# Causal masks of a state-space mixer by matmul: 64-token blocks against 32-token blocks

## The chip, the core and the metric

The kernel runs on one core of a Trainium2 chip. The metric is device time in microseconds, from the first to the last instruction of the program with the little that lies around it. Five engines matter: TensorE (PE, with the weight loads listed apart as PEld), VectorE (DVE), ScalarE (ACT), GpSimd (POOL) and SyncE (SP), which issues most of the DMAs.

## The reference

The input is 4 sequences of 1024 tokens with 512 features. It passes a mixer a, a feed-forward gate, a mixer b and the same gate again, each with a residual sum. Both mixers are state-space layers. With `a = A * dt` per token and head, the part that matters here is the decay between a token `s` and a later token `l` of a chunk, and its use:

```python
A_cs = jnp.cumsum(Ac, axis=-1)
L = jnp.exp(segment_sum(Ac))          # exp(sum of a over s < k <= l), 0 where l < s
Gm = jnp.einsum('bclhn,bcshn->bclsh', Cc, Bc)
M = Gm * jnp.transpose(L, (0, 2, 3, 4, 1))
Y_diag = jnp.einsum('bclsh,bcshp->bclhp', M, hc)
```

`segment_sum` holds minus infinity where `l < s`, so that a token takes nothing from later ones. Mixer a has 16 heads and mixer b 64. Mixer b is written in the reference as a scan over tokens; the kernel computes both in chunks of 128 tokens.

## The kernel before

The program is mixer a, the feed-forward part, mixer b, the feed-forward part again. A mixer runs over 4 sequences with 4 groups of two chunks of 128 tokens each: 16 groups, 32 chunks. While a group's chunks are worked off (`chunk`, L736), the projections of the next group run between them (`front`, L420: `convolve` with matmuls at L324 and taps on DVE at L451, `gate` with L518), and the normalisation of the one after it. The order of PE, DVE, ACT and POOL is written out by hand: `chunk` yields the us that it holds as covered, and a loop (L966 to L980) puts in pieces of `front` for that time. Each engine takes its instructions strictly in that order. Small matmuls (transposes, `pd`, `misc`) are slipped in between the large ones.

Per chunk, `decays(t)` (L755) makes the decays of 16 heads: once per chunk in mixer a, four times (t = 0 to 3) in mixer b, 160 times in all. It takes four PSUM banks `sg[r]`, each of 128 tokens `s` by 4 heads by 128 tokens `l`. First come the mask products (L762): an identity in bf16 times `later`, a matrix with -32768 where `l < s`, in two diagonal blocks of 64 by 64 tokens per bank, each with `start=True`. Then one matmul per bank (L772) adds `past` times `upto`, in f16: 21 rows for each r, at partitions 32 r to 32 r + 20. In rows 0, 1, 10 and 11 `upto` holds the sums of `a` up to `l` and `past` a constant; in rows 2 to 9 and 12 to 19 `past` holds the sums up to `s` and `upto` picks the head. The rows of sums are filled for every chunk by DMAs of `lay_sums` (L618). Row 20 is constant: 1 in `past` for `s >= 64` and -32768 in `upto` for `l < 64`, so the quarter of the square that lies wholly in the forbidden half is masked by the sums themselves. The quarter with `s < 64` and `l >= 64` needs no mask.

After it, ACT takes the exponential of each bank into L (L779), DVE multiplies L by Gm (`weigh`, L786) and PE multiplies it by the inputs (`inner`, L802) into one bank `py`, of which there is one. `open_y` (L833) puts the part from the state in first, `close_y` (L850) takes `py` out on DVE. `tail` (L646, L647) is the output projection of the chunk before. All PSUM tiles but `py` come from one pool of 7 banks, so a matmul into a new bank can wait for the engine that reads the bank's last use.

The constants are built once per mixer, ahead of the loop: `flags` (L271 to L284) are 11 reductions over the identity that give columns with ones at chosen partitions, and with these DVE fills two copies of `past` (L288, L291) and of `upto` (L294, L295), the latter per t. `past` is [128, TS, 128] and `upto` [128, TS, 4, 128] with TS = 1 in mixer a and 4 in mixer b. Other DVE work stands around them in the same queue: the scaling of the convolution's weights (L244), of `Ab` (L247, L249) and of the output weights (L252), which wait for their DMAs.

## Time and profile before

| | |
|---|---|
| median of 3 runs | 3233.39 us (3232.75 to 3239.16) |
| profiled execution | 3234.7 us, its span 3233.0 us |
| granted TensorE clock | 0.965 mean |
| PE busy | 2890.7 us (89%), 18372 matmuls |
| DVE busy | 2035.7 us (63%) |
| ACT, POOL busy | 1246.2 us (39%), 782.5 us (24%) |
| mask products L762, mixer b / a | 1024 / 256 matmuls, mean 277 / 279 ns |
| sums L772, mixer b / a | 512 / 128 matmuls, mean 386 / 390 ns |

The matmuls of mixer a run from about 72 to 1240 us, those of mixer b from about 1422 to 2951; the feed-forward parts lie between and after. In a row of the timeline, the numbers are the start in us from the span's start and the us from the first start to the last end of a run of like instructions; an idle time in brackets names what ended it. Matmuls are pipelined, so the mean of one is longer than the distance from one to the next, which is read from the starts. In a row of a group of instructions, busy time and mean of one come first, and then the idle time of that engine just ahead of it. A wait is put down to the last instruction that it waited for.

### The profile page before, as it was taken

How to read it: one execution, taken by the hardware profiler on the slowest of the kernel's cores; microseconds unless marked ns; L12 is line 12 of the kernel's file. 1: busy time of each engine (PE TensorE's matmuls, PEld its weight loads, DVE VectorE, ACT ScalarE, POOL GpSimd, SP SyncE). 2: the span in 40 equal slices, each digit the busy share in tenths (PEclk: the TensorE clock that was granted, in tenths of full speed). 3: DMA queues.
4: the chain of work that ended last, by engine and by line, in shares of the span. 5: the costliest groups of instructions: out<-in, count | busy, mean ns of one | idle time of the engine just before them, and what ended most of it. 6: DMA issues, size and time to landing. Idle time of an engine off the chain costs nothing. (4 is left out here: it accounts for less than half of the span.)

```text
span 3233.0 us, 48622 instructions
## 1 busy us (share of the span) xinstructions
PE 2890.7 (89%) x18372; PEld 1916.6 (59%) x18372; DVE 2035.7 (63%) x4326; ACT 1246.2 (39%) x2848; POOL 782.5 (24%) x842
## 2 busy tenths in 40 slices
PE   6999999999999988988999888989888989997973
PEld 5666666666666653356666666666666666664331
DVE  4666566655556642267766687776687676674288
ACT  2333333333333323334443444344444444343242
POOL 1122121122211221022222223221222222221068
PEclk9999999999999998999999999999999999998987
DMA  3000000000000025420000000000000000023143
GB/s 110 15 16 15 16 16 16 22 16 16 15 16 22 16 67 176 168 86 12 29 19 25 19 26 24 19 22 22 19 25 22 17 25 19 22 68 125 33 147 117
DMA packets 100521, 135.97 MB, mean 42 GB/s; under 512 B 40792, under 2 KB 44376, under 8 KB 100288
## 3 DMA queue, kind: packets, MB, share of 16 engines
q1 hardware_dynamic: 86944, 100.92, 10.1%
q10 hardware_dynamic: 9216, 16.78, 1.4%
q0 software_dynamic: 4128, 15.16, 1.3%
q8 instruction: 146, 2.39, 0.3%
q14 instruction: 87, 0.71, 0.1%
HBM read 96.09 MB, written 36.72 MB: 41 GB/s over the span
## 5 line engine op out<-in xcount | busy, mean ns | idle before, releaser
L324 PE MATMUL pc_b<-xnT_b,w_in_b 128*128 128x259 f32 x1280 | 360.3, 408 | 22.2 <-DVE u_b L451 22.2
L786 DVE TENSOR_TENSOR L_b<-L_b,Gm_b 128x1024 f32<-128x1024 f32 x256 | 317.4, 1282 | 2.9 <-ACT L_b L779 2.9
L646 PE MATMUL pout_a<-w_out_a,h_a 128*128 128x512 f32 x512 | 285.6, 650 | 27.3 <-DVE u_a L451 27.3
L324 PE MATMUL pc_a<-xnT_a,w_in_a 128*128 128x259 f32 x1152 | 309.2, 393 | 0.0
L324 PE MATMUL pz_a<-xnT_a,w_in_a 128*128 128x256 f32 x1024 | 300.2, 407 | 8.9 <-ACT xnT_a L413 8.9
L324 PE MATMUL pz_b<-xnT_b,w_in_b 128*128 128x256 f32 x1024 | 292.4, 394 | 0.7 <-ACT xnT_b L413 0.7
L324 PEld LDWEIGHTS pc_b<-xnT_b,w_in_b 128*128 128x128 f32 x1280 | 230.7, 201 | 101.6 <-issue 37.3
L1141 PE MATMUL g_ps<-gw,xnT_f 128*128 128x512 f32 x512 | 253.2, 639 | 39.4 <-ACT xnT_f L1138 25.5
L779 ACT ACTIVATE L_b<-seg_b 128x512 f32<-128x512 f32 x512 | 262.7, 598 | 65.9 <-PE seg_b L772 65.1
L646 PE MATMUL pout_b<-w_out_b,h_b 128*128 128x512 f32 x512 | 278.5, 635 | 0.0
L451 DVE SCALAR_TENSOR_TENSOR u_b<-pc_b,cw_b,u_b 128x256 f32<-128x256 f32 x480 | 231.7, 483 | 70.7 <-ACT u_b L447 59.3
L802 PE MATMUL py_b<-L_b,hdt_b 128*32 128x128 f32 x4096 | 162.7, 294 | 118.0 <-DVE L_b L786 116.7
L451 DVE SCALAR_TENSOR_TENSOR u_a<-pc_a,cw_a,u_a 128x256 f32<-128x256 f32 x432 | 208.3, 482 | 53.0 <-ACT u_a L447 41.6
L324 PEld LDWEIGHTS pc_a<-xnT_a,w_in_a 128*128 128x128 f32 x1152 | 193.3, 190 | 68.5 <-issue 22.9
L802 PEld LDWEIGHTS py_b<-L_b,hdt_b 128*32 128x32 f32 x4096 | 109.5, 115 | 161.7 <-issue 81.7
L1141 PEld LDWEIGHTS g_ps<-gw,xnT_f 128*128 128x128 f32 x512 | 97.4, 201 | 169.2 <-issue 116.4
L324 PEld LDWEIGHTS pz_a<-xnT_a,w_in_a 128*128 128x128 f32 x1024 | 168.6, 193 | 47.1 <-ACT xnT_a L413 9.3
L447 ACT ACTIVATE u_a<-pc_a,cb_a,cw_a 128x256 f32<-128x256 f32 x144 | 81.3, 564 | 283.9 <-PE pc_a L324 220.3
L324 PEld LDWEIGHTS pz_b<-xnT_b,w_in_b 128*128 128x128 f32 x1024 | 166.3, 190 | 37.1 <-issue 18.2
L854 POOL TENSOR_TENSOR h_b<-h_b,z_b 128x256 f32<-128x256 f32 x128 | 90.6, 729 | 386.4 <-ACT sq_b L853 386.4
L824 DVE TENSOR_TENSOR yo_a<-po_a,ea_a 128x512 f32<-128x512 f32 x56 | 36.1, 686 | 220.4 <-PE po_a L820 220.4
L647 PEld LDWEIGHTS ssq_a<-ones,sq_a 128*128 128x128 f32 x512 | 98.4, 194 | 127.8 <-issue 115.9
(310 smaller groups left out, 5275.3 us busy)
## 6 DMA issues: line engine op xcount, KB each, us to landing
x_f<-xa SPq DMA_DIRECT2D x32, 256.0 KB
sgd<-sg SPq DMA_DIRECT2D x32, 256.0 KB
sgl<-sgd SPq DMA_DIRECT2D x32, 256.0 KB
x_b<-xa SPq DMA_DIRECT2D x32, 256.0 KB
xb<-x_b ACTq DMA_DIRECT2D x32, 256.0 KB
x_f<-xb SPq DMA_DIRECT2D x32, 256.0 KB
x_g<-xb SPq DMA_DIRECT2D x32, 256.0 KB
out<-x_g SPq DMA_DIRECT2D x32, 256.0 KB
```

The source lines that it names most:

```text
L324: nc.tensor.matmul(*args, **kw)
L447: nc.scalar.activation(u, ps[:, 0:GT], AF.Identity, bias=cb[:, j : j + 1], scale=cw[:, j, 0:1])
L451: nc.vector.scalar_tensor_tensor(u, ps[:, k : k + GT], cw[:, j, k : k + 1], u, ALU.mult, ALU.add)
L646: nc.tensor.matmul(pout, f.hs[e // 2][:, e % 2, cols], w_out[:, e, :], **on)
L647: nc.tensor.matmul(ssq[:, 0:1], sqs[e // 4][:, e % 4, :], ones[:, 0:1], **on)
L779: nc.scalar.activation(L[:, r], sg[r0 + r], AF.Exp)
L786: nc.vector.tensor_mul(Lr, Lr, Gm.unsqueeze(1).to_broadcast([P, 2 * HB, P]))
L802: nc.tensor.matmul(py[cg * CT : (cg + 1) * CT, e % 4, :], hdt[:, h // HC, u : u + HC, :], Ls[half][:, r, hq, :], start=not started[cg], st ...
L824: nc.vector.tensor_mul(heads_of(tmp), heads_of(po), over_head(el[:, half * HALF : (half + 1) * HALF], P, HALF))
L854: nc.gpsimd.tensor_mul(yh, yh, zs[half * 2 + r][:, :, cols])
L1141: nc.tensor.matmul(ps, xnT[:, k, :], gw[:, k, :], start=(k == 0), stop=(k == KD - 1))
```

## The change

The mask products now come in four diagonal blocks of 32 by 32 tokens per bank instead of two of 64 by 64: 16 matmuls of 128 columns per call of `decays` instead of 8 of 256. What lies in a 64-token block off these diagonal blocks and is forbidden (`s` in 32 to 63 with `l` in 0 to 31, and `s` in 96 to 127 with `l` in 64 to 95) is masked by two more constant rows, 21 and 22, of `past` and `upto`. The sums' matmuls therefore read 23 rows instead of 21. `flags` gets two more columns, `past` two more steps per copy and `upto` two more steps per copy and t. Line numbers below L305 stay as they were.

```diff
-            flags = wk.tile([P, 2 * HB + 3], F32, tag="flags", name=f"flags_{m.name}")
+            flags = wk.tile([P, 2 * HB + 5], F32, tag="flags", name=f"flags_{m.name}")
...
-                + [slice(20, 21)]
+                + [slice(20 + n, 21 + n) for n in range(3)]
...
+            steps = [(slice(0, 64), slice(64, P)), (slice(0, 32), slice(32, 64)), (slice(64, 96), slice(96, P))]
+            steps = [(flags[:, 2 * HB + 2 + n : 2 * HB + 3 + n], *at) for n, at in enumerate(steps)]
...
-                nc.vector.tensor_scalar(past[:, :, 64:], past[:, :, 64:], row20, None, ALU.add)
+                for on, _, s in steps:
+                    nc.vector.tensor_scalar(past[:, :, s], past[:, :, s], on, None, ALU.add)
...
-                    nc.vector.scalar_tensor_tensor(
-                        upto[:, t, :, :64],
-                        row20.unsqueeze(1).to_broadcast([P, HB, 64]),
-                        MASKED,
-                        upto[:, t, :, :64],
-                        ALU.mult,
-                        ALU.add,
-                    )
+                    for on, l, _ in steps:
+                        to = upto[:, t, :, l]
+                        spread = on.unsqueeze(1).to_broadcast([P, HB, l.stop - l.start])
+                        nc.vector.scalar_tensor_tensor(to, spread, MASKED, to, ALU.mult, ALU.add)
...
-                        for q in range(2):
-                            at = slice(64 * q, 64 * q + 64)
+                        for q in range(4):
+                            at = slice(32 * q, 32 * q + 32)
                             nc.tensor.matmul(
                                 sg[r][at, :, at],
                                 ident16[at, at],
-                                later[at, at].unsqueeze(1).to_broadcast([64, HB, 64]),
+                                later[at, at].unsqueeze(1).to_broadcast([32, HB, 32]),
...
-                        rows = slice(32 * r, 32 * r + 21)
+                        rows = slice(32 * r, 32 * r + 23)
```

More of the change, by code (lines that the diff above doesn't have):

```diff
@@ L274, in mixer @@
                 + [slice(10 * lo, 10 * lo + 2) for lo in (0, 1)]
-                + [slice(20, 21)]
+                + [slice(20 + n, 21 + n) for n in range(3)]
             ):
                 nc.vector.tensor_reduce(flags[:, i : i + 1], eye[:, :, at], mybir.AxisListType.XY, ALU.add)
-            heads4, first2, row20 = flags[:, :HB], flags[:, 2 * HB : 2 * HB + 1], flags[:, 2 * HB + 2 :]
+            heads4, first2 = flags[:, :HB], flags[:, 2 * HB : 2 * HB + 1]
             nc.vector.scalar_tensor_tensor(
```

## The prediction

> **What bounds the kernel now.** I read the granted clock first (0.965 on the one core, 1.0 in the stretches used below), then the busy digits: PE is busy 89% of the span, DVE 63%, ACT 39%, POOL 24%. PE is the fullest engine, but its matmul time is not evenly the limit, so next came the waits of PE alone, to see where it stands still in the two mixers:

> ```profile
> PE py_b L802 <- DVE L_b L786: 116.7, 75, 5.2
> PE pout_a L646 <- DVE u_a L451: 27.3, 14, 3.0
> PE pc_b L324 <- DVE u_b L451: 22.2, 15, 1.5
> ```

> The columns are us in total, times, longest. There are 16 groups of two chunks in each mixer, so a row with 14 or 15 times is a wait that comes back in nearly every group, always for DVE. A PE instruction that ends earlier ahead of such a wait makes only the wait longer. So I laid one group of mixer b out in time: PE's rows with the mask products (L762) and each wait behind them (columns: start, us, instruction, idle time before it).

> ```profile
> 1846.78 0.62 PE L762 MATMUL seg_b<-later,ident 64*64 64x256 bf16 x8
> ...
> 1861.70 0.62 PE L762 MATMUL seg_b<-later,ident 64*64 64x256 bf16 x8
> ...
> 1866.37 0.62 PE L762 MATMUL seg_b<-later,ident 64*64 64x256 bf16 x8
> ...
> 1870.63 0.64 PE L802 MATMUL py_b<-L_b,hdt_b 128*32 128x128 f32 x16 [0.92 <-DVE L_b L786]
> ...
> 1891.39 2.21 PE L802 MATMUL py_b<-L_b,hdt_b 128*32 128x128 f32 x32 [5.24 <-DVE L_b L786]
> ...
> 1897.74 0.62 PE L762 MATMUL seg_b<-later,ident 64*64 64x256 bf16 x8
> 1898.29 0.40 PE L772 MATMUL seg_b<-upto_b,past_b 21*128 21x512 f16 x4
> ...
> 1900.06 0.35 PE L647 MATMUL ssq_b<-ones,sq_b 128*128 128x1 f32 x2 [0.31 <-DVE u_b L451]
> ...
> 1911.49 0.62 PE L762 MATMUL seg_b<-later,ident 64*64 64x256 bf16 x8
> 1912.05 0.40 PE L772 MATMUL seg_b<-upto_b,past_b 21*128 21x512 f16 x4
> 1913.92 0.68 PE L324 MATMUL pc_b<-xnT_b,w_in_b 128*128 128x259 f32 x2 [1.48 <-DVE u_b L451]
> ```

> What the reader is to see: from 1846.78 to 1861.70 PE has no idle time, while in DVE's rows a z_b of L518 stands at 1862.40 and waits for the gate that PE made just before 1861.70. From there DVE runs with one short gap (1.02 at 1874.01, itself behind DVE's own Gm_b) to 1898.4, and PE waits for it three times. So PE leads in one stretch of the group and DVE in the next.

> **The change part by part.** (1) The mask products. A narrow window around 1898 shows the pairs of one block one by one:

> ```profile
> 1897.87 0.49 PE L762 MATMUL seg_b<-later,ident 64*64 64x256 bf16 x6
> ...
> 1898.09 0.27 PE L762 MATMUL seg_b<-later,ident 64*64 64x256 bf16 x2
> ```

> The first of the eight starts at 1897.74, the third at 1897.87, the seventh at 1898.09: two pairs take 0.22, so a pair takes 0.109 us for 256 columns in each of two 64x64 tiles at once. The sums (L772) start 0.20 after the last pair: 0.109 of it is that pair, 0.09 the switch of the array from 64 rows to 32. The four sums of 386 ns each start together and end within 0.40. After the change there are four quads of 128 columns in four 32x32 tiles instead of four pairs of 256 columns. If a quad takes half a pair's time, a block saves 4 x (0.109 - 0.055) = 0.22 us. No row of before shows 32x32 tiles, so the bounds are: a quad that takes 0.109 saves nothing; quads that run one matmul after the other cost 16 x 0.055 = 0.87 against 0.44, a loss of 0.44; at best the switch to the sums goes too, since both would then be 32 rows high, and a block saves 0.31. I take 0.22 by the two nearest rows: the sums run in four row tiles at once, and at 1883.12 the 32 L802 matmuls (four column tiles, 128 columns of f32) take 1.01 until the next start, less a switch of 0.10 some 0.114 per quad. The eight 259-column f32 matmuls of L324 at 1909.64 take 1.85 to the next start, 0.09 of it a switch: 0.22 each, twice as long per column as bf16, so L802's quad runs at the full rate of its columns. Two more rows in the sums (23 for 21) cost nothing: their time goes by 512 columns; past and upto keep their shape and the DMAs that fill the rows of sums are unchanged, so SP's queue is too.

> [...] By the row, both tiles of a pair write the bank sg[r] and still start and end together (eight matmuls of 0.27 in 0.62). [...]

> (2) Which of the 160 blocks count. Mixer b, eight blocks per group: those at 1861.70 and 1866.37 end in the waits of 0.92 and (1872.84) 1.56 for L_b, the one at 1879.36 in the 5.24, the one at 1897.74 in the 0.31, that at 1911.49 in the 1.48, that at 1918.19 in waits of 0.61 and 0.49. In each, DVE's run began earlier than the block, so the saving turns into wait. Two are left: the last of the second chunk (1929.70; PE then runs to 1941 with no wait above 0.2 while DVE waits 1.34 for py_b) and the first of the next group (as at 1846.78). That is 32 in 16 groups, and I add 2 for the last chunks, where no projections of a next group fill PE. Mixer a, two blocks per group: PE has no wait between the first (505.18) and 521.2, where DVE's next run starts; the second is followed by the wait that the second row above counts:

> ```profile
> 541.41 0.62 PE L762 MATMUL seg_a<-later,ident 64*64 64x256 bf16 x8
> 541.97 0.39 PE L772 MATMUL seg_a<-upto_a,past_a 21*128 21x512 f16 x4
> ...
> 544.05 1.10 PE L646 MATMUL pout_a<-w_out_a,h_a 128*128 128x512 f32 x2 [1.69 <-DVE u_a L451]
> ```

> So 16 in a, 50 in all: 50 x 0.22 = 11.0 us less.

> (3) Setup on DVE, once per mixer. Mixer b at 1419 to 1432:

> ```profile
> 1419.24 0.87 DVE L277 TENSOR_REDUCE flags_b<-ident 128x1 f32<-128x8 f32 x11
> ...
> 1422.17 0.18 DVE L244 TENSOR_SCALAR cw_b<-cw_b 128x40 f32<-128x40 f32 x1 [0.33 <-DMA cw_b<-in_L_attn_b_conv_w]
> ...
> 1430.94 0.75 DVE L295 SCALAR_TENSOR_TENSOR upto_b<-flags_b,upto_b 128x256 f16<-128x256 f32 x2
> 1431.73 0.06 DVE L308 MEMSET sign_b<- 64x1 f32 x1
> 1431.82 0.36 DVE L488 TENSOR_TENSOR v_b<-pd_b,dtb_b 128x64 f32<-128x64 f32 x2
> ```

> DVE goes without a gap worth naming from here to 1464.8; PE's pd_b for the L488 was done by 1428.3, PE waits 8.77 for xn_b at 1453 and 1.46 for parts_b at 1461, and the first sums at 1473 wait for the DMA behind two_b. So DVE work added here moves everything after it. Added: 2 reductions at 0.07 (0.87 for 11) = 0.15; 4 more past steps of 128 elements, from L291 (next start 0.15 after 64 elements, 0.20 after 256) at 0.17 = 0.7; 16 more upto steps of 128 elements. L295 gives 0.335 from start to start for 256 elements, about 0.07 fixed and 0.27 for the elements, so 0.20 for 128: 3.2; where each waits for the one before (four dependent L542 of 128 take 1.27) 0.32: 5.1. Together 4.0 to 6.0; I take 4.5. DVE idles 0.33 for cw_b and 0.91 for Ab_b (1425.20) among them, and what stands ahead of those takes their place: 1.2 off, so 3.3 more, between 2.8 and 6.0. In mixer a the same comes to 10 instructions, some 1.7 us, at 6 to 9 us. What hides them is ACT: the second copy of xnT stands behind the exponential of Ab_a, which waits for its DMA until 20.1, so 8 us of cover; without it they would cost the 1.7.

> Sum: 3234.7 (the profiled execution: span 3233.0 and 1.7 around it) - 11.0 + 3.3 = 3227.0. That execution is 1.3 above the median of the runs, so on the median's scale 3225.7.

> **The rivals.** (A) Issue bounds the quads. Each matmul brings its own weight load, and no row keeps up 20 matmuls faster than L802's 28 ns each; 16 x 28 = 0.45, as long as the pairs now. For it: nothing shorter is sustained in this trace. Against: the sums' four loads and matmuls start within about 0.01 of each other. Then only the setup is left: +3.3, 3236.7. (B) Fewer blocks count: DVE and PE are close where I took PE to lead (L3's second half is weighed at 1937.28, its product starts near 1938.2, so 0.9 in hand, which speaks against). With 32 blocks: -7.0 + 3.3, 3229.7. [...] (D) Every block counts, 160 x 0.22 = 35, less 3.3: 3201.6; the waits shown speak against it.

> **How the numbers follow.** Forecast 0.60, A 0.15, B 0.08, C 0.11, D 0.06. About 0.2%, 6.5 us, is what a measurement of this kernel can tell from no change. The forecast's own range: saving per block 0.20 to 0.31, 46 to 54 blocks, setup 2.8 to 6.0, so 3220 to 3230; some three quarters of it lie below 3226.9. Faster: 0.45 from it and D's 0.06, 0.51. Same: the rest of it, A and B, 0.37. Slower: C and a little of A, 0.12. Leaving out C and D (0.17), the range is 3219 to 3239.

> **What would show it.** L762 with 2560 matmuls of 32*32 32x128, a block some 0.34 from its first mask to its sums instead of 0.55, and 0.66 to the matmul after the sums instead of 0.88. The wait of py_b for L_b grows from 116.7 by some 14 (four blocks per group), that of pout_a from 27.3 by 3. The last upto step of mixer b ends about 3.3 later after its first reduction. [...] The prediction is wrong if the groups move by other than 0.44 in b and 0.22 in a, or if the DMA waits do not cover part of the setup.

## The result, and the profile after

| | before | after |
|---|---|---|
| median of 22 runs each | 3236.72 us (3229.52 to 3242.47) | 3244.88 us (3233.86 to 3253.35) |
| ratio to before, 95% interval | | 1.0022 (1.0013 to 1.0030) |
| profiled execution: its time, its span | 3234.7, 3233.0 us | 3247.1, 3245.4 us |
| granted TensorE clock, profiled execution | 0.965 | 0.957 |
| granted TensorE clock, mean of the runs that list it (before: those beside the experiments) | 0.963 | 0.958 |

The kernel became slower by 0.22%, some 8 us on the medians. The forecast was 3225.7 against the 3233.39 known then, faster by 0.24%, with a range that ended at 3239: sign and range were both wrong.

Where the time went is read from the starts of four fixed points in the two traces, in us: the first and the last block of mask products in each mixer, and on DVE the first reduction of `flags_b` and the first z_b (L518) of mixer b. "Half" counts the stretches of 3.41 us with a granted clock of 0.5, in mixer a between 150 and 1170 us, in mixer b between 1500 and 2900 us.

| | before | after | difference | forecast |
|---|---|---|---|---|
| mixer a, first to last block (half) | 1124.2 (5) | 1134.7 (13) | +10.5 | -3.5 |
| setup of b, first reduction to first z_b | 12.85 | 16.68 | +3.8 | +3.3 |
| mixer b, first to last block (half) | 1474.2 (23) | 1473.8 (29) | -0.4 | -7.5 |
| the rest of the span | 621.7 | 620.2 | -1.5 | 0 |

Mixer a, where the forecast had the smaller saving, makes most of the loss; mixer b gains almost nothing; the setup is as forecast. The page of the changed kernel, its head and its clock digits:

```profile
span 3245.4 us, 51214 instructions
PE 2892.6 (89%) x19652; PEld 1917.7 (59%) x19652; DVE 2040.9 (63%) x4358; ACT 1245.7 (38%) x2848; POOL 781.4 (24%) x842
PEclk9999999999999998998999999999999999998997
```

PE has 1280 more matmuls and the same busy time as before (2890.7): busy time does not show the loss, since matmuls at half clock count as busy too (PE is busy for 3.42 of the 3.42 us of the stretch at clock 0.50 from 545.13, shown below). Now the waits of PE that the prediction read (us in total, times, longest):

```profile
PE py_b L802 <- DVE L_b L786: 121.7, 82, 5.3
PE pout_a L646 <- DVE u_a L451: 26.5, 14, 2.9
PE pc_b L324 <- DVE u_b L451: 25.5, 15, 1.7
```

The first grew by 5.0 where +14 was forecast, the second fell by 0.8 where +3 was forecast: a block that gets shorter ahead of a wait lengthens the wait, so part of these blocks did not get shorter. The timeline of PE in one group of mixer b shows which (start, us, instruction, idle time before it):

```profile
1858.62 0.40 PE L762 MATMUL seg_b<-later,ident 32*32 32x128 bf16 x16
1858.96 0.65 PE L772 MATMUL seg_b<-upto_b,past_b 23*128 23x512 f16 x4
1859.54 1.13 PE L646 MATMUL pout_b<-w_out_b,h_b 128*128 128x512 f32 x2
...
1873.58 0.40 PE L762 MATMUL seg_b<-later,ident 32*32 32x128 bf16 x16
1873.91 0.39 PE L772 MATMUL seg_b<-upto_b,past_b 23*128 23x512 f16 x4
1874.24 0.70 PE L324 MATMUL pc_b<-xnT_b,w_in_b 128*128 128x259 f32 x2
1874.78 0.38 PE L707 MATMUL misc_b<-Cc_b,Bc_b 128*128 128x128 f32 x2
...
1903.27 2.22 PE L802 MATMUL py_b<-L_b,hdt_b 128*32 128x128 f32 x32 [5.30 <-DVE L_b L786]
...
1909.91 0.40 PE L762 MATMUL seg_b<-later,ident 32*32 32x128 bf16 x16
1910.24 0.65 PE L772 MATMUL seg_b<-upto_b,past_b 23*128 23x512 f16 x4
```

The block at 1873.58 is what the prediction drew: 0.33 from the first mask to the sums, 0.66 to the next matmul. The blocks at 1858.62 and 1909.91 are the first ones (t = 0) of a chunk. Their masks are as short, but the four sums, which in 155 of the 160 blocks of before started within 0.01 of each other and ended within some 0.40, now take 0.65, and the next matmul comes 0.92 after the first mask: later than the 0.88 of before. Over all groups the medians from the first mask to the next matmul are, in us:

| block | before | after |
|---|---|---|
| mixer b, t = 0, both chunks of a group | 0.88 | 0.92 |
| mixer b, t = 1 and 2 of the first chunk, t = 2 and 3 of the second | 0.88 | 0.66 |
| mixer b, t = 3 of the first chunk: waits for DVE fall between its masks | 1.90 | 1.83 |
| mixer b, t = 1 of the second chunk: a wait for DVE follows | 2.44 | 2.44 |
| mixer a, first chunk of a group (its only block) | 0.88 | 0.84 |
| mixer a, second chunk: a wait for DVE follows | 2.64 | 2.63 |

The instructions of the block at 1909.91, with those of PE's sequencer, show why (start, length in ns):

```
1909.904  first weight load of the masks, the first mask at 1909.906
1909.928  51  sequencer, L772 EVENT_SEMAPHORE
1910.039  51  sequencer, L772 EVENT_SEMAPHORE
1910.094      last of the 16 masks starts
1910.164  51  sequencer, L772 EVENT_SEMAPHORE
1910.241      first sum starts
1910.272      second sum starts
1910.290  51  sequencer, L772 EVENT_SEMAPHORE
1910.398      third sum starts
1910.416  51  sequencer, L772 EVENT_SEMAPHORE
1910.524      fourth sum starts
```

The sums' waits for the DMAs of their rows stand as instructions of their own in PE's sequencer. There are 304 of them at L772 in both kernels, of 51 ns each in the median; in the group looked at, five belong to the first block of each chunk and none to the others, as the rows of `past` and `upto` are filled once per chunk. In the block of before at 1897.74 they ran from 1895.476 to 1896.131, some two microseconds ahead of the block: there the sequencer was that far ahead of the array. Ahead of the waits in the block stand 16 instructions there, 8 weight loads and 8 masks of 256 columns. Behind the 32 instructions for masks of 128 columns the sequencer reaches the first of the waits 0.02 us after the first mask has started, and the last sums then come 0.126 apart behind it. That, and the clock in mixer a, are the two causes that the experiments had to test.

The setup on DVE, from the timeline of the changed kernel:

```profile
1428.43 1.00 DVE L277 TENSOR_REDUCE flags_b<-ident 128x1 f32<-128x8 f32 x13
...
1431.74 0.18 DVE L244 TENSOR_SCALAR cw_b<-cw_b 128x40 f32<-128x40 f32 x1 [0.92 <-DMA cw_b<-in_L_attn_b_conv_w]
...
1444.24 0.82 DVE L302 SCALAR_TENSOR_TENSOR upto_b<-flags_b,upto_b 128x256 f16<-128x256 f32 x3
...
1445.11 0.68 DVE L518 SCALAR_TENSOR_TENSOR z_b<-tz_b,pz_b 128x512 f32<-128x512 f32 x1
```

From the first reduction to the first z_b it is 16.68 against 12.85. Of the two idle times for DMAs that I let the new work cover (0.33 for cw_b, 0.91 for Ab_b), the second is gone, but the first grew to 0.92: 0.3 in all was covered, not 1.2, so the work itself came to 4.1, below my 4.5.

### The profile page after: what moved, and what is told of

Same layout as the page of the kernel before. It is cut to its first block, busy times and chain, and to the rows that moved or that the text cites. A ratio compares the mean times of both kernels' runs of the same rounds, so it can differ in the third digit from the quotient of the medians.

```text
span 3245.4 us, 51214 instructions
## 1 busy us (share of the span) xinstructions
PE 2892.6 (89%) x19652; PEld 1917.7 (59%) x19652; DVE 2040.9 (63%) x4358; ACT 1245.7 (38%) x2848; POOL 781.4 (24%) x842
## 3 DMA queue, kind: packets, MB, share of 16 engines
q10 hardware_dynamic: 9216, 16.78, 1.4%
## 5 line engine op out<-in xcount | busy, mean ns | idle before, releaser
L324 PE MATMUL pc_b<-xnT_b,w_in_b 128*128 128x259 f32 x1280 | 363.0, 409 | 25.5 <-DVE u_b L451 25.5
L646 PE MATMUL pout_a<-w_out_a,h_a 128*128 128x512 f32 x512 | 297.6, 674 | 26.5 <-DVE u_a L451 26.5
L786 DVE TENSOR_TENSOR L_b<-L_b,Gm_b 128x1024 f32<-128x1024 f32 x256 | 317.3, 1281 | 2.7 <-ACT L_b L779 2.7
L324 PE MATMUL pc_a<-xnT_a,w_in_a 128*128 128x259 f32 x1152 | 311.3, 395 | 0.0
L324 PE MATMUL pz_a<-xnT_a,w_in_a 128*128 128x256 f32 x1024 | 300.1, 407 | 8.7 <-ACT xnT_a L413 8.7
L324 PEld LDWEIGHTS pc_b<-xnT_b,w_in_b 128*128 128x128 f32 x1280 | 232.6, 202 | 106.0 <-issue 39.1
L324 PE MATMUL pz_b<-xnT_b,w_in_b 128*128 128x256 f32 x1024 | 292.4, 394 | 0.7 <-ACT xnT_b L413 0.7
L646 PE MATMUL pout_b<-w_out_b,h_b 128*128 128x512 f32 x512 | 278.5, 635 | 0.0
L451 DVE SCALAR_TENSOR_TENSOR u_b<-pc_b,cw_b,u_b 128x256 f32<-128x256 f32 x480 | 231.5, 482 | 71.8 <-ACT u_b L447 60.4
L802 PE MATMUL py_b<-L_b,hdt_b 128*32 128x128 f32 x4096 | 163.9, 296 | 123.7 <-DVE L_b L786 121.7
L451 DVE SCALAR_TENSOR_TENSOR u_a<-pc_a,cw_a,u_a 128x256 f32<-128x256 f32 x432 | 208.3, 482 | 52.6 <-ACT u_a L447 41.6
L324 PEld LDWEIGHTS pc_a<-xnT_a,w_in_a 128*128 128x128 f32 x1152 | 194.9, 191 | 69.2 <-issue 22.9
L802 PEld LDWEIGHTS py_b<-L_b,hdt_b 128*32 128x32 f32 x4096 | 110.5, 116 | 167.4 <-issue 80.9
L324 PEld LDWEIGHTS pz_a<-xnT_a,w_in_a 128*128 128x128 f32 x1024 | 168.6, 193 | 47.1 <-ACT xnT_a L413 9.1
L324 PEld LDWEIGHTS pz_b<-xnT_b,w_in_b 128*128 128x128 f32 x1024 | 166.4, 190 | 37.1 <-issue 17.6
L647 PEld LDWEIGHTS ssq_a<-ones,sq_a 128*128 128x128 f32 x512 | 102.7, 202 | 134.5 <-issue 122.5
```

The source lines that it names most:

```text
L324: nc.tensor.matmul(*args, **kw)
L451: nc.vector.scalar_tensor_tensor(u, ps[:, k : k + GT], cw[:, j, k : k + 1], u, ALU.mult, ALU.add)
L646: nc.tensor.matmul(pout, f.hs[e // 2][:, e % 2, cols], w_out[:, e, :], **on)
L647: nc.tensor.matmul(ssq[:, 0:1], sqs[e // 4][:, e % 4, :], ones[:, 0:1], **on)
L786: nc.vector.tensor_mul(Lr, Lr, Gm.unsqueeze(1).to_broadcast([P, 2 * HB, P]))
L802: nc.tensor.matmul(py[cg * CT : (cg + 1) * CT, e % 4, :], hdt[:, h // HC, u : u + HC, :], Ls[half][:, r, hq, :], start=not started[cg], st ...
```

## The experiments

The theories, as they came up. S: the first blocks lose the saving because the sums' waits are no longer met ahead of time. H: mixer a got slower through the granted clock. Rivals: that the setup is the loss; that the shorter blocks gain nothing anywhere; that something else in a's blocks is slower.

**One part alone.** The setup alone: three steps of masking and 23 rows, but blocks of 64; then the blocks of 32 with their rows in one mixer only.

```diff
 # e1_setup_alone, against the changed kernel
-for q in range(4):
-    at = slice(32 * q, 32 * q + 32)
+for q in range(2):
+    at = slice(64 * q, 64 * q + 64)
...
-        later[at, at].unsqueeze(1).to_broadcast([32, HB, 32]),
+        later[at, at].unsqueeze(1).to_broadcast([64, HB, 64]),
 # e2_b_alone ("b") and e2x_a_alone ("a"), against the changed kernel
+BLK = 32 if m.name == "b" else 64
+if BLK == 64:
+    steps = steps[:1]
...
-for q in range(4):
-    at = slice(32 * q, 32 * q + 32)
+for q in range(P // BLK):
+    at = slice(BLK * q, BLK * q + BLK)
...
-        later[at, at].unsqueeze(1).to_broadcast([32, HB, 32]),
+        later[at, at].unsqueeze(1).to_broadcast([BLK, HB, BLK]),
...
-rows = slice(32 * r, 32 * r + 23)
+rows = slice(32 * r, 32 * r + 20 + len(steps))
```

> The setup and the 23 rows alone; the mask products stay in 64-token blocks. Theory (three terms: DVE setup, sums' waits in the queue, clock gate in mixer a): from the first reduction of flags_b to the first z_b 16.7 us as in the changed kernel (12.85 before), every block from first mask to sums 0.557 and 0.88 long as before, mixer a from its first block to its last within 3 us of before's 1124 us, the total about +3.8, 0.1% slower. Rival (the 23 rows or the rows' extra masks disturb the sums): first blocks longer than 0.88 with the sums spread over 0.28 us, and mixer a about 10 us longer without any 32-token block.

> 32-token blocks in mixer b alone; mixer a has before's 64-token blocks and 21 rows. Theory (the clock gate in mixer a makes the loss): mixer a back at 1124 us within 3 us, with about 5 half-clock windows between 150 and 1170 us instead of 13; setup of b +3.8; mixer b within 2 us of before (the first blocks of the chunks 0.92, the others 0.66); total +2 to +5 against before. Rival (the loss of some 10 us comes with the new blocks wherever they are, by issue or by switches of the array): mixer b shows it too and the total stays near +8.

> 32-token blocks in mixer a alone, mixer b as before. Theory (the loss sits in mixer a's clock): mixer a 1130 to 1136 us with 9 or more half-clock windows, setup of b 12.85 as before, mixer b 1474 us; total +4 to +10 against before, so most of the whole change's loss. Rival (the loss is spread over setup and mixer b, and mixer a's windows are chance of one execution): total within 3 us of before.

| | mixer a (half) | setup of b | mixer b (half) | ratio to before, 95% |
|---|---|---|---|---|
| e1_setup_alone | 1124.3 (6) | 16.70 | 1476.3 (25) | 0.9998 (0.9988 to 1.0007) |
| e2_b_alone | 1128.5 (9) | 16.80 | 1476.8 (30) | 1.0002 (0.9992 to 1.0012) |
| e2x_a_alone | 1131.4 (11) | 13.17 | 1474.7 (23) | 1.0013 (0.9999 to 1.0027) |

The setup of 3.8 us is there in each trace with the new steps in b, but not in e1's total: +3.8 was expected, and the interval, -3.9 to +2.3 us, leaves it out. What made up for it is not shown. In e1's trace the blocks take 0.88 as before and the sums stay together, so the 23 rows do not spread them; nor is one sum longer with 23 rows, 384 ns in the median in mixer b of the changed kernel for 385 before. With blocks of 32 in b alone the total is that of before. The blocks in a alone are slower in the point estimate, with an interval that just reaches one. In mixer a the same code gave 1124.2, 1124.3 and 1128.5 us with 5, 6 and 9 half-clock stretches (before, e1, e2), the changed code 1134.7 and 1131.4 with 13 and 11: a's time follows the number of stretches, which differs between executions too, and a single trace needs care here.

**The sums first.** The sums open the accumulation and the masks close it. The sums' waits then have no block of masks between the projections and themselves.

```diff
 # e3_sums_first, against the changed kernel: in decays(t)
+for r in range(4):
+    rows = slice(32 * r, 32 * r + 23)
+    nc.tensor.matmul(sg[r], past[rows, t, :], upto[rows, t], start=True, stop=False, skip_group_check=True)
 for r in range(4):
     for q in range(4):
...
-            start=True,
-            stop=False,
+            start=False,
+            stop=True,
-for r in range(4):
-    rows = slice(32 * r, 32 * r + 23)
-    nc.tensor.matmul(sg[r], past[rows, t, :], upto[rows, t], start=False, stop=True, skip_group_check=True)
```

> The changed kernel with the order within a block turned round: the four sums first (they open the bank), then the sixteen mask products. Theory (the sums' waits for DMA stand behind 32 mask instructions, so the sequencer comes to them too late): the four sums start within 0.02 us of each other in all blocks with landed DMAs, blocks of 0.66 instead of 0.92 or 0.84, 0.25 us less in 32 blocks on PE's stretch, 5 to 8 us in all as far as the clock gate lets them through; half-clock windows in mixer a as many as in the changed kernel (13) or more. Rival (the spread of the sums comes from the array, four row tiles with 23 rows after 32x32 tiles): the spread of 0.28 stays in the first blocks of the chunks, and so does the time.

Ratio to before 0.9997 (0.9986 to 1.0008); mixer a 1134.1 (10), setup 16.77, mixer b 1463.5 (25). The timeline of PE in e3, one group of mixer b with the first block of each chunk at 1856.31 and 1908.66:

```profile
1856.31 0.39 PE L761 MATMUL seg_b<-upto_b,past_b 23*128 23x512 f16 x4
1856.64 0.40 PE L767 MATMUL seg_b<-later,ident 32*32 32x128 bf16 x16
1856.97 1.13 PE L646 MATMUL pout_b<-w_out_b,h_b 128*128 128x512 f32 x2
...
1871.01 0.40 PE L761 MATMUL seg_b<-upto_b,past_b 23*128 23x512 f16 x4
1871.33 0.40 PE L767 MATMUL seg_b<-later,ident 32*32 32x128 bf16 x16
1871.67 0.70 PE L324 MATMUL pc_b<-xnT_b,w_in_b 128*128 128x259 f32 x2
...
1908.66 0.40 PE L761 MATMUL seg_b<-upto_b,past_b 23*128 23x512 f16 x4
1908.99 0.40 PE L767 MATMUL seg_b<-later,ident 32*32 32x128 bf16 x16
1909.32 1.13 PE L646 MATMUL pout_b<-w_out_b,h_b 128*128 128x512 f32 x2
```

The first blocks take 0.66 to the next matmul like the rest, and mixer b is 10.7 us shorter than before, 10.3 shorter than after. The only blocks whose length differs clearly from after are the first ones of the two chunks of each group, by 0.26 each. From these blocks to the next ones it is 0.30 and 0.18 less on average, which in 16 groups is 7.7 of the 10.3. So S holds for b; the 2.6 left over are not explained. Mixer a is as long as in after: its loss is another one. The block of each group's first chunk is even longer there, 1.16 to the next matmul, as its sums now wait openly for the DMAs of the rows.

**The clock in mixer a.** The timeline of the changed kernel at the wait behind a's second block, the place that the prediction showed of before at 541.41:

```profile
541.85 0.40 PE L762 MATMUL seg_a<-later,ident 32*32 32x128 bf16 x16
542.18 0.74 PE L772 MATMUL seg_a<-upto_a,past_a 23*128 23x512 f16 x4
544.48 1.40 PE L646 MATMUL pout_a<-w_out_a,h_a 128*128 128x512 f32 x2 [1.55 <-DVE u_a L451]
...
545.96 2.06 PE L646 MATMUL pout_a<-w_out_a,h_a 128*128 128x512 f32 x2
...
549.39 1.10 PE L646 MATMUL pout_a<-w_out_a,h_a 128*128 128x512 f32 x2
```

After the wait a pair of L646 takes 1.40 and then 2.06, until it is back at the 1.10 that before had at once (at 544.05). The busy times by stretches of 3.41 us, here and one group later (length, then busy us of PE, PEld, DVE, ACT, POOL with counts, the granted clock, DMA share, GB/s):

```profile
541.72:545.13 3.41, 1.86 (x23) 0.80 (x22) 3.27 (x6) 2.70 (x8) 0.97 (x1) 1.00 0.00 0
545.13:548.55 3.42, 3.42 (x9) 2.13 (x8) 2.83 (x10) 1.59 (x4) 0.00 (x0) 0.50 0.00 0
616.81:620.23 3.42, 1.78 (x23) 0.80 (x22) 2.07 (x5) 2.71 (x9) 0.00 (x0) 1.00 0.00 0
620.23:623.64 3.41, 3.41 (x9) 1.75 (x7) 3.02 (x10) 1.78 (x4) 0.00 (x0) 0.50 0.00 0
```

In the clock records of both traces (64 and 92 of them) every change between 1.0 and 0.5 lies a whole number of 3.413 us from the others, so the clock is read here by stretches of 3.41 us on one grid. If each matmul is counted for as long as its columns stream (259 columns of f32 in 0.22, 128 of bf16 in 0.056), the full-clock stretches of mixer a that were followed by half clock streamed some 0.29 to 0.40 of the time in before and 0.32 to 0.47 in after; of those that were not, the emptiest had 0.40 and 0.43. In the two together, every such stretch under 0.40 was followed by half clock and none over 0.47; between, both occur. This count gives no sharper limit, and the stretch with a's second block and the wait of 1.7 behind it, some 0.43 at 541.72 in after, lies in between. Whether the shorter masks pushed it over is for the experiments to show.

Two more things follow from the grid. Eleven of the 13 half-clock stretches of after begin 75.1 us apart, at 319.9, 394.9, 470.0, 545.1 and so on to 1070.8, once per group: 75.1 is 22 stretches. A slowed group thus ends with its wait at the same place of the grid, and the next one is slowed too. And a stretch at clock 0.5 costs up to half of its 3.41 us, 1.7 us by my estimate, if PE sets the pace. The experiment: make the masks of a's second block several times. They are written with `start=True`, so the result is that of the last time; the additional products fill the wait.

```diff
 # e4_after_fill_a, against the changed kernel: in decays(t)
-for r in range(4):
-    for q in range(4):
+for _ in range(7 if m.name == "a" and c == 1 else 1):
+    for r in range(4):
+        for q in range(4):
 # e5_before_fill_a: the same in the kernel before, with range(4 if ... else 1)
 # e6_before_fill_ab: e5, and ahead of the wait of 5.24 in mixer b, 18 products of zeros into py
+for _ in range(18 if c == 0 else 0):
+    nc.tensor.matmul(py, later[:, P - 1 :].to_broadcast([P, P]),
+                     ident16.unsqueeze(1).to_broadcast([P, 4, P]), start=False, stop=False,
+                     skip_group_check=True)
```

> The changed kernel with the sixteen mask products of the second chunk of every group of mixer a issued seven times (each repeat opens the bank anew, so nothing adds up): 96 more matmuls and some 1.34 us more of PE time in each of 16 groups, ahead of a wait of 1.7 to 3 us. Theory (the gate halves the clock because PE streams too little in a window of 3.4 us around that wait): the half-clock windows of mixer a go from 13 to at most 2, mixer a gets 10 to 16 us shorter than in the changed kernel, groups of 73.7 us instead of 75.1, although PE does 21 us more work; total some 10 us below the changed kernel. Rival (the loss is PE time, not clock): mixer a stays as long or gets longer by up to 21 us.

> The kernel before with its eight mask products of the second chunk of every group of mixer a issued four times: 24 more matmuls, 1.3 us of PE time ahead of the wait of 1.7 us, and nothing of the change. Theory (the clock gate, not the 32-token blocks as such, costs the time): also here the half-clock windows of mixer a go from about 5 to at most 2 and mixer a from 1124 to some 1117 us, total 5 to 9 us below before. Rival (the gate matters only with the changed blocks): mixer a stays at 1124 us or gets longer.

> As the run with mixer a filled, and in mixer b 18 matmuls of zeros of 128 by 512 columns (0.22 us each, 3.9 us per group) that add nothing to the open bank, in the first chunk of every group just ahead of the product with L3, where PE waits 5.2 us for DVE. Theory (half clock after that wait makes PE's catch-up slower, 1.1 to 1.7 us per window): the half-clock windows of mixer b go from 23 to under 8 and mixer b gets 10 to 25 us shorter. Rival (DVE sets the pace there, the clock behind the wait is hidden): fewer half-clock windows, but mixer b within 4 us of 1474 us.

| | mixer a (half) | mixer b (half) | ratio to before, 95% |
|---|---|---|---|
| after | 1134.7 (13) | 1473.8 (29) | 1.0022 (1.0013 to 1.0030) |
| e4_after_fill_a | 1116.9 (2) | 1476.2 (30) | 0.9982 (0.9973 to 0.9991) |
| before | 1124.2 (5) | 1474.2 (23) | 1 |
| e5_before_fill_a | 1114.8 (0) | 1474.3 (23) | 0.9976 (0.9966 to 0.9985) |
| e6_before_fill_ab | 1117.4 (1) | 1474.9 (4) | 0.9979 (0.9971 to 0.9988) |

With more products to make, mixer a becomes 17.8 us shorter in the changed kernel and 9.4 in the one before, and with the filling the two differ by 2.1 where they differed by 10.5. So H holds: the loss in a goes with the half clock, 1.6 and 1.9 us for each stretch that is gone (17.8 for 11, 9.4 for 5). The 1.9 is above the 1.7 that a stretch can cost, so some of the 9.4 has another source. The longest waits of PE in e5 hold no row of pout_a for u_a any more, since the additional masks fill most of it (at 540.50 it is 0.37, for 1.69 at 544.05 of before):

```profile
PE py_b L803 <- DVE L_b L787: 117.0, 75, 5.2
PE g_ps L1142 <- ACT xnT_f L1139: 25.5, 20, 3.5
PE py_a L834 <- DVE h_a L851: 25.3, 17, 4.6
PE pc_b L324 <- DVE u_b L451: 22.2, 15, 1.5
```

In mixer b of the kernel before, the 19 stretches of half clock that e6 took away had cost nothing. The busy table of e6, for 150 to 1170 and for 1500 to 2900 us, has the clock at 1.00 in b (before: 0.97), and b lasts as long as before (1474.9 against 1474.2), not 10 to 25 us less: the rival holds, behind the wait of 5.24 it is DVE that sets the pace.

```profile
150.00:1170.00 1020.00, 992.96 (x5841) 704.16 (x5841) 624.06 (x1491) 371.43 (x933) 201.14 (x268) 1.00 0.06 18
1500.00:2900.00 1400.00, 1298.32 (x9999) 887.17 (x9998) 999.80 (x1969) 595.41 (x1385) 362.56 (x353) 1.00 0.08 25
```

**Is it the lost streaming?** e4 shows what half clock costs, not why the change brought more of it. The shorter masks stream 0.22 us less in a's second block, which is 0.065 of a stretch; the sums' spread is a rival. So the masks of that block were made just twice: as much streaming as with blocks of 64, the sums still spread.

```diff
 # e11_after_masks_twice_a, against e4
-for _ in range(7 if m.name == "a" and c == 1 else 1):
+for _ in range(2 if m.name == "a" and c == 1 else 1):
```

> The changed kernel, with the masks of mixer a's second chunk of each group made twice: 0.22 us of extra products in a block that is followed by the wait for the taps, so that PE streams in that block and wait for as long as with the blocks of 64 tokens. The four sums still start spread over 0.28 us. Theory 1 (the lost 0.22 us of streaming makes the additional half-clock windows of mixer a): 4 to 9 windows of half clock in mixer a, which takes 1121 to 1129 us from its first to its last block; the time 0.9990 to 1.0012 of the kernel before. Theory 2 (the spread of the sums, or something else that the masks' length does not touch, makes them): 10 to 13 windows, 1131 to 1136 us, the time 1.0013 to 1.003. In both the setup stays at 16.7 and mixer b at 1474.

Ratio to before 1.0003 (0.9992 to 1.0014); mixer a 1124.8 (7), setup 16.72, mixer b 1476.0 (29). The ratio, mixer a and its count of stretches are all those of the first theory. The same place in its timeline:

```profile
540.64 0.62 PE L763 MATMUL seg_a<-later,ident 32*32 32x128 bf16 x32
541.20 0.52 PE L773 MATMUL seg_a<-upto_a,past_a 23*128 23x512 f16 x4
543.28 1.10 PE L646 MATMUL pout_a<-w_out_a,h_a 128*128 128x512 f32 x2 [1.55 <-DVE u_a L451]
```

The 32 masks take 0.56 to the sums, as the eight of 64x64 did, the wait stays 1.55, and L646 takes 1.10 behind it. Giving back the streaming took 9.9 us off mixer a. The spread of the sums was not held quite fixed: in the median of these blocks it is 0.15 us, for 0.28 in after. But from the first mask to the next projection it is 2.63 us in both kernels, so the spread is hidden in the wait and has no time of its own to give.

These blocks also tell what exposes the waits. Where the five waits hold up the sums, the last sum starts 0.60 us after the first wait was met (the medians of after, e4 and e11 agree). It was met 0.31 us ahead of the first sum in after, 0.36 in e4 and 0.45 in e11, and the sums spread over 0.28, 0.24 and 0.15. In e5 it was met 1.27 ahead and in before over 2, and the sums start within 0.01. Yet the sequencer led by some 20 to 45 instructions in all of them: of the loads and matmuls ahead of the sums, 21 had still to start when it met the first wait in after, 28 in e4, 44 in e11, 38 in e5 and 33 in before. So it is not the number of instructions alone: in these kernels the sums stayed together where those in the lead lasted longer than the 0.60 us of the waits (1.27 and over 2), and spread where they did not (0.31 to 0.45).

**Both remedies, and the best of them.** e8 is e3 with a's second block made seven times; e7 is e8 with the products of zeros of e6 in mixer b; e9 is the kernel before with the sums first and a's second block four times. e10 takes what was best in each mixer: a as in e5 (blocks of 64, masks first, four times in the second block), b with blocks of 32 and the sums first.

```diff
 # e10_mixed, against the changed kernel
+BLK = 32 if m.name == "b" else 64
+if BLK == 64:
+    steps = steps[:1]
...
+late = m.name == "b"
+def masks():
+    for r in range(4):
+        for q in range(P // BLK):
+            at = slice(BLK * q, BLK * q + BLK)
+            nc.tensor.matmul(
+                sg[r][at, :, at],
+                ident16[at, at],
+                later[at, at].unsqueeze(1).to_broadcast([BLK, HB, BLK]),
+                start=not late,
+                stop=late,
+                skip_group_check=True,
+            )
+if not late:
+    for _ in range(4 if c == 1 else 1):
+        masks()
 for r in range(4):
-    for q in range(4):
...
-    rows = slice(32 * r, 32 * r + 23)
+    rows = slice(32 * r, 32 * r + 20 + len(steps))
     nc.tensor.matmul(
-        sg[r], past[rows, t, :], upto[rows, t], start=False, stop=True, skip_group_check=True
+        sg[r], past[rows, t, :], upto[rows, t], start=late, stop=not late, skip_group_check=True
     )
+if late:
+    masks()
```

> The change with the sums ahead of the mask products, and the mask products of the second chunk of every group of mixer a issued seven times (they add more of the mask to places that are masked already). Theory (setup, sums' waits and the gate in mixer a are separate terms that add): setup 16.8, mixer a 1117 us with at most 2 half-clock windows, mixer b 1463 us as with the sums first alone; span some 14 us below before, total 0.3 to 0.5% faster than before. Rival (the gains stand in each other's way): 5 us or less below before.

> As the last, and the 18 matmuls of zeros per group in mixer b. Theory: if the clock behind the 5.2 us wait is on the path, another 10 to 25 us less in mixer b; if DVE sets the pace, mixer b stays at 1463 us within 4.

> The kernel before, 64-token blocks and 21 rows, with the sums ahead of the mask products and the four-fold mask products in mixer a's second chunks. It tells what the 32-token blocks are worth once the sums' waits and the gate of mixer a are out of the way. Theory (before has no exposed waits of the sums, so their place is worth nothing there): blocks 0.88 as before, mixer b 1474 us within 2, setup 12.85, mixer a 1115 to 1121; total 0.2 to 0.3% below before, so slower than the run with 32-token blocks, sums first and mixer a filled (11 us less in mixer b for 3.9 us of setup). Rival (putting the sums first is itself what gains 11 us): mixer b 1463 us here too.

> Mixer a as before, with its mask products four-fold in the second chunks; mixer b with 32-token blocks, the sums ahead of them. Theory: the terms add: mixer a 1115 to 1118 us, setup 16.8, mixer b 1463 us, span about 3218, total 0.4 to 0.5% below before, the fastest of all. Rival (the gate takes back in one mixer what is won): 0.3% or less below before.

| | mixer a (half) | setup of b | mixer b (half) | median us | ratio to before, 95% |
|---|---|---|---|---|---|
| e8_sums_first_fill_a | 1120.8 (2) | 16.72 | 1463.1 (22) | 3223.60 | 0.9964 (0.9951 to 0.9977) |
| e7_sums_first_fill_ab | 1123.4 (3) | 16.78 | 1477.5 (14) | 3235.28 | 0.9998 (0.9990 to 1.0007) |
| e9_before_sums_first_fill_a | 1127.5 (4) | 13.14 | 1473.8 (20) | 3237.88 | 0.9996 (0.9984 to 1.0009) |
| e10_mixed | 1114.2 (0) | 16.95 | 1464.7 (27) | 3218.79 | 0.9942 (0.9929 to 0.9955) |

e9 shows that the sums first are worth nothing to b with blocks of 64 (1473.8): there the waits were met ahead of time anyway, and the block is as long in either order. In a they cost, so e9's total misses the 0.2 to 0.3% expected: 1127.5 against 1114.8 in e5, and in e8 1120.8 against 1116.9 in e4. The block of a's first chunk, whose sums then stand open to the DMAs of their rows, is longer by 0.31 and 0.25 us on average, 5.0 and 4.0 in 16 groups. That covers the 3.9 of e8; of the 12.7 of e9 the rest stands beside four stretches of half clock where e5 has none. e7 misses: the products of zeros in b, which did no harm in e6, cost 14 us beside the sums first (1477.5 against 1463.1). Its waits have a row "ssq_b for u_b" of 20.6 us in 14 times, but e6 has one of 16.2 in 13 times; this stays open. e10 adds up as its parts said, a of e5 and b of e8, and is the fastest kernel here, 0.58% below before.

## Why the prediction was wrong

**The masks themselves (part 1): right.** Four 32x32 tiles write the same bank at once: in the instructions of a block at full speed the quads start 0, 67, 123 and 178 ns after the first mask (the block at 1909.91), some 0.056 to 0.067 each, where I took 0.055. From the first mask to the sums it is 0.334 us for 0.557, exactly the 0.22 forecast. Rival A (issue, a block of 0.55) is refuted. The quads do not run one matmul after the other either (part 1's bound of 0.87): the four row tiles of a quad write one bank in the 0.056 to 0.067 us that one mask of 128 columns was to take. The other bound, that the switch to the sums goes too and a block saves 0.31, is not what came: the first sum starts 0.15 us after the last mask, 0.09 more than the mask's 0.055, and in before it was 0.20 and 0.109, so 0.09 too, though masks and sums are now both 32 rows high.

**"0.66 to the matmul after the sums instead of 0.88" (part 1): wrong in every first block of a chunk.** I took everything behind the masks as unchanged, because shape and DMAs of the sums were. What I left out is that the first sums of a chunk carry five waits (four in a group's first chunk of mixer a), which take the sequencer up to 0.60 us. Behind 32 short instructions instead of 16 longer ones its lead at the first of them fell from over 2 us to 0.31, in the medians. That takes the saving from 64 of the 160 blocks: 0.92 and 0.84 for 0.88, not 0.66.

**"50 in all" (part 2): the count met the wrong blocks.** All 16 counted in mixer a are first blocks of a chunk, and so are the 16 of b that were "the first of the next group": 32 of the 50 lost their saving. Of the 11.0 us there remain the 18 others, 4.0; b showed 0.4 of them. From the last block of a group of b to the first of the next it is 0.18 us less than before on average, as the count had it (2.9 in 16 groups), but between the other blocks b gives most of it back. Whether the count itself was right cannot be read from the changed kernel. With the sums first, b gains 10.7, 0.67 per group, which is worth three blocks of 0.22 per group where I counted two. Rival B (fewer blocks count) is nearest to what b shows, shorter blocks with its groups as far apart as before (92.83 us on average, 92.87 before), but for another reason than the one it gave, and its -7.0 for 32 blocks did not come.

**The granted clock: a term that was missing.** I read the clock first, saw that it was 1.0 in the stretches I used, and named no condition on which it would stay so. The row that I showed for mixer a was the one that mattered: a block followed by a wait of 1.69. "A PE instruction that ends earlier ahead of such a wait makes only the wait longer" was my rule, and a longer wait was to cost nothing; in mixer a each stretch at half clock that came or went was worth 1.3 to 1.9 us. This term, +10.5 in the profiled execution, outweighs all others. On the medians it is smaller: e2x gives +0.13% (-0.01 to +0.27) for mixer a, some 4 us, and e11, which takes it away, stands 0.19% below after, some 6 us.

**The setup (part 3): right in size** (3.8 for 3.3), with the work a little cheaper and the cover of DMA waits smaller than I took them. It had little weight in the outcome: e1's total does not show it.

**The rivals.** None of them was what happened. The side "slower", 0.12, was all but 0.01 the chance of C, which took 0.44 more per block, the bound of part 1 for quads that run one matmul after the other. No run shows that term: the runs show 0.334 us to the sums for 0.557. The waits' place in the queue and the clock both spoke for slower and could have been read in the trace of before: the sequencer's waits at L772, two microseconds ahead of a block, and five stretches of half clock in mixer a, all behind the same wait.

## What to carry to other kernels

When one matmul is split into many, count the instructions that now stand ahead of the next matmul that waits for several transfers, and how long they last. In these kernels its waits were free only where PE's sequencer led by more time than they took, 0.60 us for five. The lead was some 20 to 45 instructions in every block looked at, which was 1.27 us of e5's long masks and 0.31 to 0.45 of short ones. Put such matmuls first where the data is there in time, and last where it is not. Work taken from PE just ahead of a wait isn't free either: look whether the stretch of 3.41 us around the wait still streams about half of the time (in mixer a of both kernels none that streamed over 0.47 of it was followed by half clock), and if not, try filling the wait with products that nobody needs. It paid in mixer a; in mixer b it gave nothing in e6 and cost 14 us in e7.
